# Two chunks' shift and exponential in one operation each, in the second attention layer of a fused kernel

## The chip, the cores and the metric

The kernel runs on one core of one Trainium2 chip. The metric is the time on the device in microseconds, as the median of several runs. One profiled execution per kernel stands beside it; its span runs from the first to the last instruction. In views of the profile, PE is the matrix engine (TensorE), PEld its loading of weights, DVE is VectorE, ACT is ScalarE, POOL is GpSimd and SP is the engine whose queue issues most DMAs. L944 is line 944 of the kernel before.

## The reference

The input x has two images of 256 channels and 64 x 64 places, in fp32. Two attention layers follow each other. The change lies in the second one ("layer 1"), which takes the first one's output:

```python
def _L1_conv_ref(x, w_qkv, b_qkv, w_out, b_out):
    import jax
    import jax.numpy as jnp
    HEADS = 4
    b, c, h, w = x.shape
    head_dim = c // HEADS
    qkv = jnp.einsum('oc,bchw->bohw', w_qkv, x) + b_qkv[None, :, None, None]
    qkv = qkv.reshape(b, HEADS, 3 * head_dim, h * w)
    q, k, v = jnp.split(qkv, 3, axis=2)
    scale = 1.0 / jnp.sqrt(jnp.asarray(head_dim, x.dtype))
    attn = jax.nn.softmax(jnp.einsum('bhdn,bhdm->bhnm', q, k) * scale, axis=-1)
    out = jnp.einsum('bhnm,bhdm->bhnd', attn, v).reshape(b, c, h, w)
    return jnp.einsum('oc,bchw->bohw', w_out, out) + b_out[None, :, None, None] + x
```

There are 4 heads of 64 channels and 4,096 places, so each head of each image has a 4,096 x 4,096 matrix of scores, which goes through a softmax along the keys. Layer 0 is an attention of the same kind with 4 heads of 16 channels, a normalisation ahead of it and a gate behind it.

## The kernel before

**Tiling.** Layer 1 works in 32 units: two images, two pairs of heads, and eight blocks of 512 queries. A unit runs over 32 chunks of 128 keys. For each chunk, keys lie along the partitions, and a tile of 128 x (2 heads x 512 queries) holds the scores. A step handles two chunks, so a unit has 16 steps and the layer 512. A unit is cut into two halves of 16 chunks (8 steps): each half has its own maximum per query, its own values' sums and its own sum of weights, and the two are joined at the end.

**The path of one chunk.** PE multiplies keys by queries into a pair of PSUM banks (`score`, L861). There are two such pairs, so the scores of a step's first chunk and of its second chunk each reuse the pair of the same chunk of the step before. VectorE takes the running maximum with the pair (`keep`, L878), and ScalarE copies the pair into an SBUF tile of 128 x 1024 fp32, called `raw` (L879). When a half is done, its maximum is turned across the partitions by PE (`turn_max`, L886), reduced by VectorE (`fold`, L898), split by GpSimd into three bf16 numbers (`split`, L909 to L916), turned back (`turn`, L925) and spread over all partitions in one pair of PSUM banks (`spread_shift`, L939). From then on, each chunk of the half gets this negative maximum added by VectorE in place (`shift`, L944), goes through the exponential on ScalarE in place (in `weigh`, L956), is added into the sum of weights by GpSimd (also in `weigh`, L966 for the first addition of a half and L968 for the others), and is multiplied by the values on PE (`gather`, L978). The last ten odd chunks (and two even ones) get their sums of weights on PE instead (L988).

**The delay.** `LAG` is 10 steps: a chunk's shift comes 10 steps after its scores. The even chunk is shifted and weighed in the same step; the odd chunk is shifted at that step's end and weighed at the next one's beginning. Both are gathered 11 steps after their scores. The `raw` tiles live in a ring of 24 (2 x LAG + 4).

**The order.** All of it is written out by hand: `seq` keeps instructions in program order, so each engine's queue is the order in which the loop at L1219 to L1247 issues. A step first issues the scores of both chunks, then the weights of the old odd chunk, then the first chunk's maximum and copy, the even chunk's shift and weights, then the second chunk's maximum and copy, then the values' sums of two chunks, and last the odd chunk's shift. Other work hangs at named places of a step ("start", "early", "early end", "late", "late end") through `at` (L1109 to L1156): the projections of the next queries and of the next keys and values (the latter for 24 of the 32 units, kept in DRAM in between), the turning of maxima at steps 0 and 8 of a unit, the sums of weights, factors and rows of the unit before at steps 12 to 14, and the output projection of the first image. After the last scores, `fetch_last`, `last_output` and `project_half` bring x and the attention rows in and form the second image's output.

The core of a step, with the middle left out:

```python
            if 0 <= t - LAG - 1 < END:
                weigh(pair[1] - 2 * LAG - 2)
...
            if inside:
                keep(pair[0], scores[0])
            if behind:
                shift(pair[0] - 2 * LAG)
                weigh(pair[0] - 2 * LAG)
...
            if inside:
                keep(pair[1], scores[1])
```

Of the kernel before, what the change touches and what calls it, by code (L numbers as in the profile page):

```python
# [27 lines left out]
def conv_attention_kernel(  # L28
# [216 lines left out]
    with own0:  # L245
# [155 lines left out]
        def maxima(x, g):  # L401

            u = b, j = units0[x // NM]
            m, i = divmod(x % NM, PB)
            if u not in mxs:
                mxs[u] = small.tile([P, PB * H, NJ], F32, tag="mx0", name=f"mx0_{b}_{j}")
            for h in (2 * g, 2 * g + 1):
                r = slice(32 * h, 32 * h + 32)
                ps = bank(f"a0_{b}_{j}_{x % NM}_{h}")
                seq(nc.tensor.matmul(  # L410
                    ps, qs0[u][r, bass.ts(i, P)], kTs[b][r, bass.ts(m, NB)],
                    start=True, stop=True,
                ))
                seq(nc.vector.tensor_reduce(mxs[u][:, i * H + h, m : m + 1], ps, AX.X, ALU.max))  # L414
# [363 lines left out]
    with (  # L778
# [4 lines left out]
        tc.tile_pool(name="psm", bufs=1, space=PSUM) as psm,  # L783
    ):
        own_ring = ExitStack()
        ring = own_ring.enter_context(tc.tile_pool(name="ring", bufs=2 * LAG + 4))
        small_bank[0] = lambda name: psm.tile([P, NB], F32, tag="misc", name=name)
        rmax, negs, mrows, shifts, raws, accs = {}, {}, {}, {}, {}, {}
        avs1, srows, losts, joined, halves = {}, {}, {}, {}, {}
        rts = [None, None]  # L790
        outs = {}
        halves_of = {}
        kd, vd = (
# [73 lines left out]
        def keep(t, ps):  # L867

            u = b, g, j = units[t // NM]
            m = t % NM  # L870
            raw = ring.tile([P, 2, NB], F32, tag="raw", name=f"raw_{b}_{g}_{j}_{m}")
            raws[t] = raw
            n = m // GS
            if m > 0:
                before = raws[t - 1] if m == 1 else rmax[u, (m - 1) // GS]
                if (u, n) not in rmax:
                    rmax[u, n] = l1.tile([P, 2, NB], F32, tag="rmax", name=f"rmax_{b}_{g}_{j}_{n}")
                seq(nc.vector.tensor_tensor(rmax[u, n], ps, before, ALU.max))  # L878
            seq(nc.scalar.copy(raw, ps))  # L879
# [61 lines left out]

        def shift(t):
            u = units[t // NM]
            seq(nc.vector.tensor_tensor(  # L944
                raws[t], raws[t], shifts[u, t % NM // GS], ALU.add
            ))

        def on_tensor(t):
            return t >= LATE and (t % 2 == 1 or t < LATE + 4)
# [1 line left out]
        def weigh(t):  # L951
            u = b, g, j = units[t // NM]
            m = t % NM
            n = m // GS
            p = raws[t]
            seq(nc.scalar.activation(p, p, AF.Exp, scale=D1**-0.5))  # L956

            if on_tensor(t):
                return
            if (u, n) not in first:  # L960
                first[u, n] = p
            elif (u, n) not in accs:
                accs[u, n] = l1.tile(
                    [P, 2, NB], F32, tag="acc", bufs=3, name=f"acc_{b}_{g}_{j}_{n}"
                )
                seq(nc.gpsimd.tensor_tensor(accs[u, n], first[u, n], p, ALU.add))  # L966
            else:
                seq(nc.gpsimd.tensor_tensor(accs[u, n], accs[u, n], p, ALU.add))  # L968
# [43 lines left out]

        def keep_total(u):
            b, g, j = u
            row = l1.tile([P, NB], F32, tag="srow", bufs=1, name=f"srow_{b}_{g}_{j}")
            seq(nc.scalar.copy(row, srows[u]))
            srows[u] = row
            seq(nc.scalar.activation(losts[u], losts[u], AF.Exp, scale=D1**-0.5))
# [78 lines left out]
                )  # L1097

        def fetch_output(b, j):
            fetch(("xo", b, j), x1[b][j], "xo", 2, l1)  # L1100
            fetch(("ao", b, j), att[b][:, bass.ts(j, NB)], "ao", 1, l1)


# [5 lines left out]
        for n, u in enumerate(units):  # L1109
            b, g, j = u  # L1110
            t0 = n * US
            if n > 0:
                at(t0 - 5, "start", lambda u=u, b=b, j=j: fetch(("q", u), x1[b][j]))
                at(t0 - 2, "late", lambda u=u: next_queries(u, 0))
                at(t0 - 1, "early", lambda u=u: next_queries(u, 1))
                at(t0 - 1, "early end", lambda u=u: keep_queries(u))
            if n < len(units) - NJ:
                to = (*units[n + NJ][:2], j)
                at(t0 + 1, "start", lambda to=to: fetch(("kv", *to), x1[to[0]][to[2]]))
                for c in range(CC):  # L1120
                    at(t0 + 4 + c, "early", lambda to=to, c=c: next_keys(*to, c))
                at(t0 + 5, "early end", lambda to=to: store_keys(*to))
                at(t0 + 6, "early", lambda to=to: next_values(*to, 0))
                at(t0 + 7, "early", lambda to=to: next_values(*to, 2))
                at(t0 + 7, "early end", lambda to=to: store_values(*to))

                t1 = (n // NJ * NJ + NJ - 1) * US
                at(t1 + 2 * j + 2, "start", lambda to=to: load_keys(*to))
                at(t1 + 2 * j + 3 + LAG, "start", lambda to=to: load_values(*to))
            for k in range(NG):  # L1130
                t1 = t0 + (k + 1) * GS // 2
                at(t1, "early", lambda u=u, k=k: turn_max(u, k, 0))
                at(t1, "early end", lambda u=u, k=k: fold(u, k, 0))
                at(t1, "late", lambda u=u, k=k: turn_max(u, k, 1))
                at(t1, "late end", lambda u=u, k=k: (fold(u, k, 1), split(u, k)))
                at(t1 + 1, "late", lambda u=u, k=k: turn(u, k))
                at(t1 + 2, "early", lambda u=u, k=k: spread_shift(u, k))
            t1 = t0 + US + GS // 2
            at(t1 + 4, "early", lambda u=u: total(u))
            at(t1 + 4, "early end", lambda u=u: keep_total(u))  # L1140
            at(t1 + 5, "early", lambda u=u: turn_total(u))
            at(t1 + 5, "early end", lambda u=u: factors(u))
            at(t1 + 5, "late", lambda u=u: turn_sums(u, 1))
            at(t1 + 5, "late end", lambda u=u: rows(u, 1))
            at(t1 + 6, "early", lambda u=u: turn_sums(u, 0))
            at(t1 + 6, "early end", lambda u=u: rows(u, 0))
            if b < B - 1 and (g, j) == (PR - 1, NJ - 1):
                for i in range(NJ):
                    t1 = t0 + US + (i + 4) * GS // 2
                    at(t1, "start", lambda b=b, i=i: fetch_output(b, i))  # L1150
                    for o in range(CC):
                        at(
                            t1 + 3 + 4 * o, ("early", "late")[o],
                            lambda b=b, i=i, o=o: project_out(b, i, o, misc(f"o1_{b}_{i}_{o}")),
                        )
                        at(t1 + 3 + 4 * o, "late end", lambda b=b, i=i, o=o: output(b, i, o))  # L1156
# [5 lines left out]
        def fetch_last(i):  # L1162

            b = B - 1
            tag, bufs, pool = (("xb", 3, l1x), ("xo", 2, l1), ("ao", 1, l1))[(i >= 3) + (i >= 5)]
            t = pool.tile([P, CC, NB], F32, tag=tag, bufs=bufs, name=f"x_last_{i}")
            nc.sync.dma_start(out=t, in_=x1[b][i].rearrange("(c p) n -> p c n", p=P))
            last_x.append(t)
# [7 lines left out]
        def last_output():  # L1176
# [7 lines left out]
                r, n = k * D1, D1 - NB // D1  # L1184
                nc.sync.dma_start(out=a[r : r + n, :], in_=att[b][P + r : P + r + n, :])
            last_att.append(a)
            for i in range(NJ - 2, NJ):
                t = tail.tile([P, CC, NB], F32, tag=f"xo{i}", name=f"x_last_{i}")
                nc.sync.dma_start(out=t, in_=x1[b][i].rearrange("(c p) n -> p c n", p=P))
                last_x.append(t)  # L1190
# [14 lines left out]
                    seq(nc.vector.tensor_tensor(x, ps[:, o, :], x, ALU.add))  # L1205

        own_tail = ExitStack()
        for i in range(NJ - 2):
            at(END - 12 + 2 * i, "start", lambda i=i: fetch_last(i))
        at(END, "start", lambda: fetch_first_half())  # L1210
        at(END + LAG, "late end", lambda: last_output())


        FILL = {
# [4 lines left out]
        for t in range(max(t for t, _ in extras) + 1):  # L1219
            inside, behind = 0 <= t < END, 0 <= t - LAG < END  # L1220
            pair = (2 * t, 2 * t + 1)
            scores = [score(c) for c in pair] if inside else []
            if 0 <= t - LAG - 1 < END:
                weigh(pair[1] - 2 * LAG - 2)
            hung(t, "start")
            hung(t, "early")
            for j in FILL.get((t, "early"), ()):
# [2 lines left out]
                keep(pair[0], scores[0])  # L1230
            if behind:
                shift(pair[0] - 2 * LAG)
                weigh(pair[0] - 2 * LAG)
            hung(t, "early end")
            for j in FILL.get((t, "early end"), ()):
                project_half(j, 0, first_half[j])
            if inside:
                keep(pair[1], scores[1])
            if 0 <= t - LAG - 1 < END:
                for c in pair:  # L1240
                    gather(c - 2 * LAG - 2)
            hung(t, "late")
            hung(t, "late end")
            for j in FILL.get((t, "late end"), ()):
                project_half(j, 0, first_half[j])
            if behind:
                shift(pair[1] - 2 * LAG)  # L1247
        assert not extras
        for j in range(NJ):
            project_half(j, 1, last_att[0][:, bass.ts(j, NB)])  # L1250
# [54 lines left out]
```

## Time and profile before

| | |
|---|---|
| median of 3 runs | 4,742.67 us (4,740.17 to 4,742.81) |
| the profiled execution | 4,741.58 us, span 4,739.8 us |
| busy over the span | PE 96%, DVE 83%, ACT 72%, POOL 54% |
| 2,900 to 3,100 us, of 200 us | PE 188.5, DVE 187.9, ACT 169.1, POOL 185.0 |
| layer 1's shifts, L944 | 1,024 of 1,213 ns |
| layer 1's exponentials, L956 | 1,024 of 1,062 ns |
| layer 1's sums of weights, L968 | 884 of 2,373 ns |

A line of a group has the program's line, the engine and the operation, the output and the inputs by name, their shapes (partitions x elements) and how many there are; then the busy time in us and the mean of one in ns; then how long the engine stood idle just before them, and which engine and line ended most of that. A line of a timeline has the start in us from the span's start, the duration, and the idle time just before it with what ended it. Consecutive instructions on VectorE overlap a little in these records (a start every 1.13 us at 1.22 us of duration), so distances between starts are safer than sums of durations. A PE row of "x4" or "x8" is a run of that many instructions.

### The profile page before, as it was taken

Reading aid. Unit: us, or ns where it says so; the run is one execution under the profiler, and the core shown is the slowest. Engines: PE = TensorE matmul, PEld = TensorE weight load, DVE = VectorE, ACT = ScalarE, POOL = GpSimd, SP = SyncE. Lnnn points to the kernel's source line nnn. Section 1 sums busy time; section 2 is a strip of 40 time slices with the busy share of each in tenths; the row PEclk is TensorE's granted clock in tenths of the full one; section 3 lists DMA queues with packets and bytes.
Section 4 is the critical chain, followed back from the end, with each engine's and each line's share of the span. In section 5 each row is a group of like instructions: output and inputs, shape, how many; then the busy total and the mean of one; then the engine's idle time right before and its main releaser. Section 6 shows DMA issues by size and latency. Waiting matters only on the chain.

```text
span 4739.8 us, 70643 instructions
## 1 busy us (share of the span) xinstructions
PE 4526.9 (96%) x27506; PEld 1496.2 (32%) x27506; DVE 3917.0 (83%) x4584; ACT 3394.1 (72%) x4508; POOL 2540.6 (54%) x1491
## 2 busy tenths in 40 slices
PE   8999999999999999989999999999999999999998
PEld 3433333333333333333232232323233332222222
DVE  6777777777777777359999999999999899999996
ACT  3366666666666666668888888888887778888884
POOL 6300000000000000039999999999998889999994
PEclk9999999999999999999999999999999999999999
DMA  3100000000000000110000100001111111000002
GB/s 103 34 4 19 19 21 15 15 15 15 15 15 15 15 13 13 57 63 25 23 25 17 54 30 23 25 23 36 52 36 45 63 52 47 18 14 7 14 16 74
DMA packets 113381, 140.10 MB, mean 30 GB/s; under 512 B 51864, under 2 KB 52696, under 8 KB 112932
## 3 DMA queue, kind: packets, MB, share of 16 engines
q1 hardware_dynamic: 111260, 135.11, 9.2%
q8 instruction: 216, 3.54, 0.3%
q14 instruction: 121, 0.99, 0.1%
q10 hardware_dynamic: 1784, 0.46, 0.0%
HBM read 93.58 MB, written 41.70 MB: 29 GB/s over the span
## 4 chain that ended last, share of the span: by engine, by line
PE 58%; DVE 15%; POOL 15%; issue 6%; ACT 5%; DMA 1%; SPq 0%; ACTq 0%; DVEq 0%; POOLq 0%
PE s L448 24%; POOL acc L968 13%; PE av L463 12%; DVE rmax L878 10%; PE s L861 6%; PE av L978 5%; DVE raw L944 4%; ACT raw L879 4%; PE a L410 2%; PE p L270 1%; PE k1p L672 1%; POOL acc L966 1%; PE rt L886 1%; PE q1p L672 1%; PE o L549 1%
## 5 line engine op out<-in xcount | busy, mean ns | idle before, releaser
L968 POOL TENSOR_TENSOR acc<-acc,raw 128x1024 f32<-128x1024 f32 x884 | 2098.1, 2373 | 89.4 <-ACT raw L956 30.2
L414 DVE TENSOR_REDUCE mx<-a 128x1 f32<-128x512 f32 x2048 | 1315.3, 686 | 450.5 <-PE a L410 449.4
L451 ACT ACTIVATE p<-s 128x512 f32<-128x512 f32 x2048 | 1109.8, 597 | 701.3 <-PE a L410 367.3
L944 DVE TENSOR_TENSOR raw<-raw,shift 128x1024 f32<-128x1024 f32 x1024 | 1238.0, 1213 | 19.2 <-PE shift L939 12.7
L861 PE MATMUL s<-q,k 64*128 64x512 f32 x4096 | 1117.2, 636 | 142.9 <-ACT raw L879 134.6
L878 DVE TENSOR_TENSOR rmax<-s,rmax 128x1024 f32<-128x1024 f32 x960 | 1170.1, 1219 | 72.7 <-PE s L861 70.8
L879 ACT COPY raw<-s 128x1024 f32<-128x1024 f32 x1024 | 1037.7, 1013 | 259.4 <-DVE rmax L878 173.5
L448 PE MATMUL s<-q,kT 32*128 32x512 f32 x4096 | 1219.1, 640 | 0.0
L956 ACT ACTIVATE raw<-raw 128x1024 f32<-128x1024 f32 x1024 | 1086.9, 1062 | 178.4 <-DVE raw L944 147.3
L410 PE MATMUL a<-kT,q 32*128 32x512 f32 x4096 | 1129.7, 643 | 1.2 <-DVE mx L414 1.0
L978 PE MATMUL av<-raw,v 128*64 128x512 f32 x4096 | 999.3, 606 | 2.0
L463 PE MATMUL av<-p,v 128*32 128x256 f32 (+1 forms) x7904 | 650.2, 399 | 0.6 <-ACT avs L477 0.6
L861 PEld LDWEIGHTS s<-q,k 64*128 64x128 f32 x4096 | 317.1, 185 | 827.9 <-ACT raw L879 628.0
L513 POOL TENSOR_TENSOR f<-f,dyn 128x16 f32<-128x16 f32 x15 | 3.3, 223 | 1028.2 <-DVE f L512 1028.2
L448 PEld LDWEIGHTS s<-q,kT 32*128 32x128 f32 x4096 | 397.9, 183 | 426.3 <-issue 392.1
L978 PEld LDWEIGHTS av<-raw,v 128*64 128x64 f32 x4096 | 243.3, 136 | 587.6 <-issue 428.8
L463 PEld LDWEIGHTS av<-p,v 128*32 128x32 f32 x7904 | 157.6, 108 | 751.5 <-issue 737.3
L564 POOL TENSOR_SCALAR res<-res 128x1024 f32<-128x1024 f32 x16 | 16.8, 1049 | 660.5 <-ACT res L563 660.5
L410 PEld LDWEIGHTS a<-kT,q 32*128 32x128 f32 x4096 | 305.0, 184 | 31.4 <-DVE mx L414 18.2
L966 POOL TENSOR_TENSOR acc<-raw,raw 128x1024 f32<-128x1024 f32 x64 | 152.4, 2381 | 112.7 <-ACT raw L956 103.8
L898 DVE TENSOR_REDUCE negs<-rt 128x4 f32<-128x512 f32 x128 | 88.3, 690 | 50.1 <-PE rt L886 47.6
L318 DVE RECIPROCAL std<-std 128x128 f32<-128x128 f32 x64 | 56.1, 920 | 37.7 <-ACT std L313 37.7
(332 smaller groups left out, 1840.4 us busy)
## 6 DMA issues: line engine op xcount, KB each, us to landing
x<-in_x_dram SPq DMA_DIRECT2D x16, 512.0 KB
res<-in_x_dram SPq DMA_DIRECT2D x16, 512.0 KB
x<-res SPq DMA_DIRECT2D x16, 512.0 KB
att<-rows SPq DMA_DIRECT2D x62, 128.0 KB
kd<-k1s SPq DMA_DIRECT2D x24, 256.0 KB
vd<-v1s SPq DMA_DIRECT2D x24, 256.0 KB
k<-kd SPq DMA_DIRECT2D x24, 256.0 KB
v<-vd SPq DMA_DIRECT2D x24, 256.0 KB
```

The costliest lines, as they stand in the source:

```text
L410: seq(nc.tensor.matmul(ps, qs0[u][r, bass.ts(i, P)], kTs[b][r, bass.ts(m, NB)], start=True, stop=True,))
L414: seq(nc.vector.tensor_reduce(mxs[u][:, i * H + h, m : m + 1], ps, AX.X, ALU.max))
L448: seq(nc.tensor.matmul(ps, kTs[b][r, bass.ts(m, P)], qs0[u][r, :], start=True, stop=True))
L451: seq(nc.scalar.activation(pt[:, k, :], ps, AF.Exp, scale=D0**-0.5))
L463: seq(nc.tensor.matmul(avs[u][32 * h : 32 * h + 32, cols], vs0[b][:, m, 32 * h : 32 * h + 32], pts[t, h // 2][:, h % 2, cols], start=(m == ...
L861: seq(nc.tensor.matmul(ps[:, k, :], ks[b, g, m // PB][r, bass.ts(m % PB, P)], qs1[u][r, :], start=True, stop=True,))
L878: seq(nc.vector.tensor_tensor(rmax[u, n], ps, before, ALU.max))
L879: seq(nc.scalar.copy(raw, ps))
L944: seq(nc.vector.tensor_tensor(raws[t], raws[t], shifts[u, t % NM // GS], ALU.add))
L956: seq(nc.scalar.activation(p, p, AF.Exp, scale=D1**-0.5))
L968: seq(nc.gpsimd.tensor_tensor(accs[u, n], accs[u, n], p, ALU.add))
L978: seq(nc.tensor.matmul(avs1[u, n][k * D1 : (k + 1) * D1, :], v[:, m % PB, k, :], raws[t][:, k, :], start=(m % GS == 0), stop=(m % GS == GS ...
```

## The change

Two neighbouring `raw` tiles become one tile of 128 x 2 x 1024, of which `keep` fills one half for each chunk. The ring holds 13 such pairs (LAG + 3). `shift` adds the negative maximum to both chunks in one VectorE operation, with the PSUM operand repeated by a stride of zero; a new function `exponentials` takes the exponential of both in one ScalarE operation. The shift of the pair stands where the even chunk's stood; behind it, the exponential and the two additions of weights belong to the pair that was shifted one step earlier. The values' sums come one step later, 12 steps behind the scores. Values are loaded, and the last output begins, one step later for that.

Room for the ring comes from other buffers: layer 0's maxima move to a pool that closes with layer 0 (two buffers, as before), the row of sums shares the keys' and values' two buffers, and the x block of the output has one buffer instead of two. So the last x blocks that are fetched early are five instead of six, and three instead of two are fetched in the tail.

```diff
-                mxs[u] = small.tile([P, PB * H, NJ], F32, tag="mx0", name=f"mx0_{b}_{j}")
+                mxs[u] = l0w.tile([P, PB * H, NJ], F32, tag="mx0", name=f"mx0_{b}_{j}")
...
-        ring = own_ring.enter_context(tc.tile_pool(name="ring", bufs=2 * LAG + 4))
+        ring = own_ring.enter_context(tc.tile_pool(name="ring", bufs=LAG + 3))
...
-            raw = ring.tile([P, 2, NB], F32, tag="raw", name=f"raw_{b}_{g}_{j}_{m}")
-            raws[t] = raw
+            if t % 2 == 0:
+                both = ring.tile([P, 2, 2, NB], F32, tag="raw", name=f"raw_{b}_{g}_{j}_{m}")
+                raw_pairs[t] = both
+                raws[t], raws[t + 1] = both[:, 0], both[:, 1]
+            raw = raws[t]
...
-            seq(nc.vector.tensor_tensor(
-                raws[t], raws[t], shifts[u, t % NM // GS], ALU.add
-            ))
+            both = raw_pairs[t]
+            by = shifts[u, t % NM // GS].unsqueeze(1).to_broadcast([P, 2, 2, NB])
+            seq(nc.vector.tensor_tensor(both, both, by, ALU.add))
+
+        def exponentials(t):
+            both = raw_pairs.pop(t)
+            seq(nc.scalar.activation(both, both, AF.Exp, scale=D1**-0.5))
...
-            seq(nc.scalar.activation(p, p, AF.Exp, scale=D1**-0.5))
...
-            row = l1.tile([P, NB], F32, tag="srow", bufs=1, name=f"srow_{b}_{g}_{j}")
+            row = l1.tile([P, NB], F32, tag="kv", name=f"srow_{b}_{g}_{j}")
...
-            fetch(("xo", b, j), x1[b][j], "xo", 2, l1)
+            fetch(("xo", b, j), x1[b][j], "xo", 1, l1)
...
-                at(t1 + 2 * j + 3 + LAG, "start", lambda to=to: load_values(*to))
+                at(t1 + 2 * j + 4 + LAG, "start", lambda to=to: load_values(*to))
...
-            for i in range(NJ - 2, NJ):
+            for i in range(NJ - 3, NJ):
...
-        at(END + LAG, "late end", lambda: last_output())
+        at(END + LAG + 1, "late end", lambda: last_output())
...
-            if 0 <= t - LAG - 1 < END:
-                weigh(pair[1] - 2 * LAG - 2)
+            old = pair[0] - 2 * LAG - 2 if 0 <= t - LAG - 1 < END else None
...
                 shift(pair[0] - 2 * LAG)
-                weigh(pair[0] - 2 * LAG)
+            if old is not None:
+                exponentials(old)
+                weigh(old)
+                weigh(old + 1)
...
-            if 0 <= t - LAG - 1 < END:
-                for c in pair:
-                    gather(c - 2 * LAG - 2)
+            if 0 <= t - LAG - 2 < END:
+                gather(pair[0] - 2 * LAG - 4)
+                gather(pair[1] - 2 * LAG - 4)
...
-            if behind:
-                shift(pair[1] - 2 * LAG)
```

More of the change, by code (lines that the diff above doesn't have):

```diff
@@ L790, in conv_attention_kernel @@
         rts = [None, None]
+        raw_pairs = {}
         outs = {}
@@ L1164, in fetch_last @@
             b = B - 1
-            tag, bufs, pool = (("xb", 3, l1x), ("xo", 2, l1), ("ao", 1, l1))[(i >= 3) + (i >= 5)]
+            tag, bufs, pool = (("xb", 3, l1x), ("xo", 1, l1), ("ao", 1, l1))[(i >= 3) + (i >= 4)]
             t = pool.tile([P, CC, NB], F32, tag=tag, bufs=bufs, name=f"x_last_{i}")
@@ L1207, in conv_attention_kernel @@
         own_tail = ExitStack()
-        for i in range(NJ - 2):
+        for i in range(NJ - 3):
             at(END - 12 + 2 * i, "start", lambda i=i: fetch_last(i))
         at(END, "start", lambda: fetch_first_half())
-        at(END + LAG, "late end", lambda: last_output())
+        at(END + LAG + 1, "late end", lambda: last_output())
         FILL = {
```

## The prediction

> **What bounds the kernel now.** The change touches layer 1, from about 2,100 us to the end. I read its costliest groups on the page first (busy us, mean ns of one, then idle time just before them and its main releaser):
>
> ```profile
> L968 POOL TENSOR_TENSOR acc<-acc,raw 128x1024 f32<-128x1024 f32 x884 | 2098.1, 2373 | 89.4 <-ACT raw L956 30.2
> L944 DVE TENSOR_TENSOR raw<-raw,shift 128x1024 f32<-128x1024 f32 x1024 | 1238.0, 1213 | 19.2 <-PE shift L939 12.7
> L861 PE MATMUL s<-q,k 64*128 64x512 f32 x4096 | 1117.2, 636 | 142.9 <-ACT raw L879 134.6
> L878 DVE TENSOR_TENSOR rmax<-s,rmax 128x1024 f32<-128x1024 f32 x960 | 1170.1, 1219 | 72.7 <-PE s L861 70.8
> L879 ACT COPY raw<-s 128x1024 f32<-128x1024 f32 x1024 | 1037.7, 1013 | 259.4 <-DVE rmax L878 173.5
> L956 ACT ACTIVATE raw<-raw 128x1024 f32<-128x1024 f32 x1024 | 1086.9, 1062 | 178.4 <-DVE raw L944 147.3
> ```
>
> Three of them wait in a ring: scores for the copy that empties their PSUM pair, the copy for the maximum of the same pair, the maximum for scores. Second, busy time by stretch (length, then PE, PEld, DVE, ACT, POOL):
>
> ```profile
> 2700.00:2900.00 200.00, 188.79 (x808) 60.75 (x810) 187.82 (x176) 169.11 (x180) 186.49 (x101) 1.00 0.10 31
> 4300.00:4500.00 200.00, 184.44 (x786) 55.26 (x784) 191.21 (x184) 170.97 (x181) 190.88 (x107) 1.00 0.05 12
> ```
>
> PE, VectorE and GpSimd are all at 92 to 96%: no engine stands alone, so the order in which they hand work to each other counts as much as the work. Third, therefore, the timeline of one engine at a time, over two steps (start us, duration us, idle before):
>
> ```profile
> 2628.66 1.13 PE L861 MATMUL s<-q,k 64*128 64x512 f32 x4
> 2630.24 1.13 PE L861 MATMUL s<-q,k 64*128 64x512 f32 x4 [0.45 <-ACT raw L879]
> 2631.29 1.13 PE L672 MATMUL k1p<-xb_('kv', 0, 1, 7)_22535,w 128*128 128x512 f32 x2
> 2632.35 1.94 PE L978 MATMUL av<-raw,v 128*64 128x512 f32 x8
> 2634.22 1.99 PE L861 MATMUL s<-q,k 64*128 64x512 f32 x8
> ```
>
> ```profile
> 2627.86 1.22 DVE L878 TENSOR_TENSOR rmax<-s,rmax 128x1024 f32<-128x1024 f32 x1
> 2628.99 1.21 DVE L944 TENSOR_TENSOR raw<-raw,shift 128x1024 f32<-128x1024 f32 x1
> 2630.12 1.22 DVE L878 TENSOR_TENSOR rmax<-s,rmax 128x1024 f32<-128x1024 f32 x1
> ...
> 2635.39 1.22 DVE L878 TENSOR_TENSOR rmax<-s,rmax 128x1024 f32<-128x1024 f32 x1 [0.66 <-PE s L861]
> 2636.53 1.21 DVE L944 TENSOR_TENSOR raw<-raw,shift 128x1024 f32<-128x1024 f32 x1
> 2637.66 1.22 DVE L878 TENSOR_TENSOR rmax<-s,rmax 128x1024 f32<-128x1024 f32 x1
> ```
>
> ```profile
> 2629.17 1.01 ACT L879 COPY raw<-s 128x1024 f32<-128x1024 f32 x1
> ```
>
> The reader is to see one **loop of two steps** in these rows. Second maximum of a step (2627.86), its copy (2629.17), the second scores of the next step, which reuse that pair (2630.24), the keys' projection, the values' sums (2632.35), the first scores of the step after (2634.22), their maximum (2635.39), a shift (2636.53), the second maximum (2637.66): 9.80 us, or 8.74 without the projection's 1.06. VectorE alone needs four starts of 1.13 us in a step, 9.04 in two. In a plain step VectorE wins (4.52 a step); where PE has a side job the loop wins, and the 0.66 us of idle VectorE is that.
>
> **What the Trainium skill says.** "VectorE: DVE Perf Modes", section on the TRN2 errata, gives an fp32 tensor_tensor (N+151)/0.96 ns: 1,224 for N = 1024, where this trace has 1,213 and 1,219; and 2,291 for N = 2048, of which the trace has none. "PSUM — Partial Sum Buffer", section on bank collisions, says that two engines may not read one bank and quadrant together and that accesses are ordered across engines for it: here every such copy starts 1.31 us or more after its maximum does, as if one needed the other's result. "Perfetto Trace Analysis", section on optimizing Scalar/DVE operations, holds both sides: larger operations help a saturated engine, and breaking instructions up helps where an engine causes bubbles on others. The trace shows VectorE in both roles.
>
> **The change part by part.**
>
> *Shift of a pair in one operation.* Two starts of 1.13 us become one of 1.13 + 1024/0.96 GHz = 2.20. At most 2.26 (nothing saved), at least 2.13 (all start cost gone). It saves VectorE 0.06 a step, 502 steps with a shift (10 to 511): 30 us, if VectorE were the bound.
>
> *Its place.* Before, the even chunk's shift stands between the two maxima and the odd one behind both. Now the whole pair stands between them. The loop passes from first to second maximum, so it gets 2.20 − 1.13 = **1.07 longer: 8.74 + 1.07 = 9.81 for two steps, 4.91 a step**, above VectorE's own 1.13 + 2.20 + 1.13 = 4.46. The second shift stood off the loop, and is now on it.
>
> *Exponentials, one step later.* A pair takes 1.06 + 1024 at 1.2 GHz = 1.92, at most 2.12. They no longer wait for a shift (147 us of waits go), but stand between the two copies: first copy at 1.31 behind the first maximum, exponential 0.97 later, done at 1.31 + 0.97 + 1.9 = 4.2 behind it; the second copy is due at 1.13 + 2.20 + 1.31 = 4.64. So 0.45 us of cover; ScalarE's side copies (0.5 to 0.7 us: k, v, q, sums) behind the exponential overrun it by about 0.1 to 0.2. The saved waits are hidden anyway.
>
> *Values' sums one step later.* Free: PE no longer waits for a fresh exponential; its order and length stay.
>
> *Ring of 13 pairs.* A first copy reuses the pair of 13 steps before, whose exponential ended about 6.9 us before that copy (two steps of 4.91 and 1.31 + 1.17, less 1.17 + 4.2). GpSimd's two sums take 2 x 2.44; about 2 us of slack are left. I take 0; if the rows' extra 2.6 us on GpSimd eat it, up to 2 us a unit.
>
> *Moved buffers.* Same counts for the layer 0 maxima: 0. The row of sums in the keys' buffers: its predecessors are five steps old, 0. One output buffer in place of two: on SP's queue the next fetch waits for a write, 1 to 4 us, three steps (15 us) before use, and nothing behind it on that queue is due sooner: 0. Keys' and values' loads a step later: as their readers, 0.
>
> *The sum, per unit (16 steps).* Units now: the sums' first small operation starts at 2596.59 and 2677.89, so 81.3 us with projections of the next keys; without, five units from 4219.94 to 4616.09 take 79.2. After: eight loops of 9.81 are 78.5. PE's side work in a unit (transposes and spreading 5.4, k 2.1, v 2.2, q 2.1, totals 1.0) is 12.8; a loop meets PE in every other step, so half, 6.4. VectorE's side work ahead of a second maximum (two reductions of 0.6, factors 0.5, rows 0.6) is 2.3: half, 1.15. A unit's first chunk has no maximum: −0.57. That is 85.5. Then places where the loop changes parity or waits for a third engine: the transposition of the maxima waits for GpSimd's split behind two sums (now up to 1.10 in the trace, twice a unit: 2.0), new queries behind the longer exponential (0.65), bank hand-over at the rows (0.3): 3.0. Walking one unit step by step with the same distances gave starts of 0, 5, 11, 15, 21, 27, 32, 38, 43, 49, 55, 59, 65, 70, 76, 82 and 88.4. **88.4 − 81.3 = 7.1 us a unit**; without projections both lose about 2.1, so it stays. 502/16 = 31.4 units: 223 us.
>
> *The end.* After the last scores PE works off the pairs left; one more is 1.87 + 0.98 = 2.9. A third x block is fetched only then, and VectorE waits for it ahead of the last rows: the first block lands 12 us after issue now; I take 4, between 0 and 6. Together 7.
>
> The profiled execution took 4,741.58 us (span 4,739.8, 1.8 around it), 1.1 below the median. 4,741.6 + 223 + 7 = 4,971.6, so **4,971**.
>
> **The rivals.**
> *A, the loop as above:* 4,971; own range 4,920 to 5,020 (5.5 to 8.6 us a unit). Chance 0.70. For it: its distances are all in one excerpt, and the loop already shows there.
> *B, side work falls into slack.* PE now idles about 0.9 us in a plain step, and if most of the side jobs hide there, a unit is 78.5 + 6 to 7, some 3.5 longer: 110 + 7, 4,859. Against: scores wait in PE's order, so a job ahead of them moves them. 0.10.
> *C, GpSimd's bursts hold the ring,* 2 us a unit more: 63, so 5,034. GpSimd is 95% busy now, but a longer step gives it rest. 0.08.
> *D, faster:* VectorE stays the bound. Then the fewer starts give 30 us less, 7 back at the end: 4,719. It decides as soon as the loop is under VectorE's 4.46 a step, that is if second scores need not wait for the second copy, by 0.45 us. For it: VectorE's 95%. Against: 0.45 us of that very wait stand in the plain step above. 0.09. That the longer operations merely trade places, near 4,742: 0.03.
>
> **How the numbers follow.** B to C leave out D and the even case, 0.12, and halves of B and C: 4,860 to 5,030. About 0.2%, 9.5 us, is what a measurement here can tell from no change: faster 0.09, same 0.03, slower 0.88.
>
> **What would show it.** Right: L944 and L956 512 times at 2.29 and 1.9 us; plain steps 4.9 apart in place of 4.52; maxima waiting for scores rising from 71 us to several hundred; VectorE's and GpSimd's shares falling to some 85%; copies waiting for maxima, not for GpSimd. Wrong: VectorE still back to back (D); plain steps of 4.9 with side jobs that add nothing (B); first copies released by GpSimd (C); a pair's shift well off 2.2.

## The result, and the profile after

The changed kernel takes **4,964.97 us** (median of 4 runs, 4,963.61 to 4,971.23) against 4,741.93 us of the kernel before on the same chip: a ratio of 1.0474, 95% interval 1.046 to 1.0488. It is slower by 223 us; the prediction said 4,971.

The same groups on the page of the changed kernel. Lines have moved: L862 is the scores, L882 the maximum, L883 the copy, L950 the shift, L954 the exponential, L975 the sums of weights.

```profile
L975 POOL TENSOR_TENSOR acc<-acc,raw 128x1024 f32<-128x1024 f32 x884 | 2093.2, 2368 | 403.0 <-ACT raw L954 359.5
L883 ACT COPY raw<-s 128x1024 f32<-128x1024 f32 x1024 | 1036.7, 1012 | 749.8 <-DVE rmax L882 711.2
L882 DVE TENSOR_TENSOR rmax<-s,rmax 128x1024 f32<-128x1024 f32 x960 | 1171.0, 1220 | 312.3 <-PE s L862 300.1
L862 PE MATMUL s<-q,k 64*128 64x512 f32 x4096 | 1135.3, 641 | 271.3 <-ACT raw L883 243.3
L950 DVE TENSOR_TENSOR raw<-raw,shift 128x2048 f32<-128x2048 f32 x512 | 1166.1, 2279 | 8.9 <-PE shift L943 7.8
L954 ACT ACTIVATE raw<-raw 128x2048 f32<-128x2048 f32 x512 | 979.2, 1914 | 1.0 <-DVE raw L950 1.0
```

Each wide operation does what was asked of it: 512 shifts cost VectorE 1,166 us in place of 1,238, 512 exponentials cost ScalarE 979 in place of 1,087, and the exponentials' waits for shifts (147 us) are gone. The time is lost in the three rows that wait in a ring: copies for maxima 711 us (174 before), maxima for scores 300 (71), scores for copies 243 (135). GpSimd now waits more as well (the additions of L975 360 us for exponentials; the same group had 30 before, and a half's first additions, L966, another 104). So every engine's share falls in the table by stretches (the same two as before):

```profile
2700.00:2900.00 200.00, 174.84 (x750) 54.73 (x750) 174.19 (x128) 149.22 (x131) 170.11 (x97) 1.00 0.12 35
4300.00:4500.00 200.00, 169.17 (x710) 50.71 (x704) 175.65 (x130) 147.85 (x127) 174.52 (x98) 0.98 0.03 8
```

And VectorE's timeline over two plain steps, with no side work on VectorE or PE (ScalarE has one small copy of 0.59 us in it):

```profile
4547.86 1.22 DVE L882 TENSOR_TENSOR rmax<-s,rmax 128x1024 f32<-128x1024 f32 x1 [0.60 <-PE s L862]
4549.01 2.28 DVE L950 TENSOR_TENSOR raw<-raw,shift 128x2048 f32<-128x2048 f32 x1
4551.20 1.22 DVE L882 TENSOR_TENSOR rmax<-s,rmax 128x1024 f32<-128x1024 f32 x1
4552.87 1.22 DVE L882 TENSOR_TENSOR rmax<-s,rmax 128x1024 f32<-128x1024 f32 x1 [0.46 <-PE s L862]
4554.02 2.28 DVE L950 TENSOR_TENSOR raw<-raw,shift 128x2048 f32<-128x2048 f32 x1
4556.21 1.22 DVE L882 TENSOR_TENSOR rmax<-s,rmax 128x1024 f32<-128x1024 f32 x1
4557.62 1.22 DVE L882 TENSOR_TENSOR rmax<-s,rmax 128x1024 f32<-128x1024 f32 x1 [0.19 <-PE s L862]
```

The shift takes 2.19 us from its start to the second maximum's, and VectorE idles for scores ahead of every first maximum. Two steps take 4557.62 − 4547.86 = 9.76 us, where the loop had been summed to 9.81, and the old kernel had 9.04. The rest of the loop, on ScalarE and PE in the same stretch:

```profile
4552.45 1.01 ACT L883 COPY raw<-s 128x1024 f32<-128x1024 f32 x1 [0.43 <-DVE rmax L882]
4553.52 1.13 PE L862 MATMUL s<-q,k 64*128 64x512 f32 x4 [1.10 <-ACT raw L883]
4554.58 1.94 PE L985 MATMUL av<-raw,v 128*64 128x512 f32 x8
4556.44 1.13 PE L862 MATMUL s<-q,k 64*128 64x512 f32 x4
```

From the second maximum (4551.20) to its copy it is 1.25 us, then 1.07 to the second scores of the next step, 1.06 to the values' sums, 1.86 to the first scores of the step after, 1.18 to their maximum (4557.62); 1.15 to the shift and 2.19 to the second maximum close the loop: 9.76. GpSimd's two additions happen to take as long as half of it (4.88 us, from starts 2.44 apart), but they don't set the pace here: GpSimd idled 2.86 and 0.17 us for exponentials ahead of the two pairs that it adds in this stretch.

### The profile page after: what moved, and what is told of

Read it like the earlier page. It is cut to its first block, busy times and chain, and to the rows that moved or that the text cites. A ratio compares the mean times of both kernels' runs of the same rounds, so it can differ in the third digit from the quotient of the medians.

```text
span 4961.8 us, 68957 instructions
## 1 busy us (share of the span) xinstructions
PE 4553.6 (92%) x27506; PEld 1502.1 (30%) x27506; DVE 3909.8 (79%) x4072; ACT 3281.9 (66%) x3996; POOL 2533.3 (51%) x1491
## 4 chain that ended last, share of the span: by engine, by line
PE 61%; DVE 12%; POOL 10%; ACT 9%; issue 5%; DMA 1%; SPq 0%; ACTq 0%; DVEq 0%; POOLq 0%
PE s L448 23%; PE av L463 12%; PE s L862 10%; POOL acc L975 9%; DVE rmax L882 8%; PE av L985 6%; ACT raw L883 4%; ACT raw L954 4%; DVE raw L950 3%; PE a L410 2%; PE p L270 1%; PE v1p L705 1%; PE k1p L672 1%; PE q1p L672 1%; PE o L549 1%
## 5 line engine op out<-in xcount | busy, mean ns | idle before, releaser
L975 POOL TENSOR_TENSOR acc<-acc,raw 128x1024 f32<-128x1024 f32 x884 | 2093.2, 2368 | 403.0 <-ACT raw L954 359.5
L883 ACT COPY raw<-s 128x1024 f32<-128x1024 f32 x1024 | 1036.7, 1012 | 749.8 <-DVE rmax L882 711.2
L882 DVE TENSOR_TENSOR rmax<-s,rmax 128x1024 f32<-128x1024 f32 x960 | 1171.0, 1220 | 312.3 <-PE s L862 300.1
L862 PE MATMUL s<-q,k 64*128 64x512 f32 x4096 | 1135.3, 641 | 271.3 <-ACT raw L883 243.3
L950 DVE TENSOR_TENSOR raw<-raw,shift 128x2048 f32<-128x2048 f32 x512 | 1166.1, 2279 | 8.9 <-PE shift L943 7.8
L954 ACT ACTIVATE raw<-raw 128x2048 f32<-128x2048 f32 x512 | 979.2, 1914 | 1.0 <-DVE raw L950 1.0
L862 PEld LDWEIGHTS s<-q,k 64*128 64x128 f32 x4096 | 315.5, 186 | 972.9 <-ACT raw L883 689.5
L410 PEld LDWEIGHTS a<-kT,q 32*128 32x128 f32 x4096 | 304.9, 183 | 31.5 <-DVE mx L414 18.2
L973 POOL TENSOR_TENSOR acc<-raw 128x1024 f32<-128x1024 f32 x63 | 148.5, 2357 | 13.8 <-ACT raw L954 12.7
L929 PE MATMUL nm1p<-ident,negmax 128*128 128x128 bf16 x256 | 25.4, 222 | 74.6 <-POOL negmax L916 74.6
```

The costliest lines, as they stand in the source:

```text
L410: seq(nc.tensor.matmul(ps, qs0[u][r, bass.ts(i, P)], kTs[b][r, bass.ts(m, NB)], start=True, stop=True,))
L862: seq(nc.tensor.matmul(ps[:, k, :], ks[b, g, m // PB][r, bass.ts(m % PB, P)], qs1[u][r, :], start=True, stop=True,))
L950: seq(nc.vector.tensor_tensor(both, both, by, ALU.add))
L954: seq(nc.scalar.activation(both, both, AF.Exp, scale=D1**-0.5))
```

## The experiments

All but the last change the order or the width of operations alone; the last changes what the maximum reads. All compute everything. Each was timed beside the kernel before, which stayed at 4,741.7 to 4,742.4 us. The distance between the first scores of one step and the next, averaged over units, is used below as "the step"; "the last units" are the 26th to the 31st, which have no projections of keys and values.

**Both shifts between the maxima, in the kernel before.** The place alone:

```diff
             if behind:
                 shift(pair[0] - 2 * LAG)
+                shift(pair[1] - 2 * LAG)
                 weigh(pair[0] - 2 * LAG)
...
-            if behind:
-                shift(pair[1] - 2 * LAG)
```

> The kernel before with one edit: the odd chunk's shift moves from the end of the step to right behind the even one's, between the two maxima; both stay single operations, exponentials, values' sums and ring as before. Loop theory (the second shift between the maxima lengthens the two-step loop through PE, VectorE and ScalarE): loop 8.74 + 1.13 = 9.87 us for two steps, 4.93 a step in place of 4.52, so about 4,975 us (4,940 to 5,010). Rival (the loss comes from the wide operations, the later exponentials and values' sums or the ring): nothing of that is in here, so 4,740 to 4,780.

Measured: 4,978.94 us, ratio 1.05 (1.0482 to 1.0517). This one moved line costs 237 us, and nothing else of the change is in this kernel. VectorE's timeline:

```profile
4304.91 1.23 DVE L878 TENSOR_TENSOR rmax<-s,rmax 128x1024 f32<-128x1024 f32 x1 [0.56 <-PE s L861]
4306.05 2.34 DVE L944 TENSOR_TENSOR raw<-raw,shift 128x1024 f32<-128x1024 f32 x2
4308.31 2.55 DVE L878 TENSOR_TENSOR rmax<-s,rmax 128x1024 f32<-128x1024 f32 x2
4310.77 2.34 DVE L944 TENSOR_TENSOR raw<-raw,shift 128x1024 f32<-128x1024 f32 x2
4313.03 1.22 DVE L878 TENSOR_TENSOR rmax<-s,rmax 128x1024 f32<-128x1024 f32 x1
4314.78 1.23 DVE L878 TENSOR_TENSOR rmax<-s,rmax 128x1024 f32<-128x1024 f32 x1 [0.53 <-PE s L861]
```

Two steps are 9.87 us, the sum that was expected. ("x2" is two instructions back to back.) The place alone makes a loss of the size that the whole change has. Whether the width, the lateness or the ring add to it is left to the runs below.

**Two single shifts in the wide one's place, in the changed kernel.** The width alone:

```diff
-            both = raw_pairs[t]
-            by = shifts[u, t % NM // GS].unsqueeze(1).to_broadcast([P, 2, 2, NB])
-            seq(nc.vector.tensor_tensor(both, both, by, ALU.add))
+            for c in (t, t + 1):
+                seq(nc.vector.tensor_tensor(
+                    raws[c], raws[c], shifts[u, t % NM // GS], ALU.add
+                ))
```

> The changed kernel with two single shifts, one behind the other, in the place of the wide one; all else as changed. Loop theory: place counts, not width: the loop is 2 x 1.13 - 2.20 = 0.06 us longer for two steps, so 4,965 to 4,995 us. Rival W (the width of the shift is the cost): a good part of the loss goes, 4,750 to 4,900.

Measured: 4,983.17 us, 18 above the changed kernel (its two runs lie 10 us apart). So the width of the shift isn't the cost; it saves a little.

**Two single exponentials in the wide one's place.** The loop in `exponentials` runs over both chunks.

> The changed kernel with two single exponentials, one behind the other, in the place of the wide one. Loop theory: 0.45 us of cover stand behind the exponential, two single ones take about 0.1 more: no change, 4,960 to 4,975 us. Rival (a pair's exponential holds GpSimd's additions back, since both chunks come at once): single ones let the first addition start 0.9 us sooner, and 20 to 60 us come back, 4,905 to 4,945.

Measured: 4,958.68 us, ratio 1.0462 (1.0444 to 1.0479), an interval that overlaps that of the changed kernel; the median is 1 us below the range expected. The width of the exponential is not the cost either, and the burst of two additions holds back next to nothing.

**The exponential ahead of the first copy, shift between the maxima.**

```diff
             scores = [score(c) for c in pair] if inside else []
...
+            if old is not None:
+                exponentials(old)
+                weigh(old)
+                weigh(old + 1)
             hung(t, "start")
...
-            if old is not None:
-                exponentials(old)
-                weigh(old)
-                weigh(old + 1)
```

> The changed kernel with the wide exponential and the additions behind it moved to the start of the step, ahead of the first copy; the wide shift stays between the maxima. Loop theory: from first maximum to second copy the shift's path is 1.13 + 2.20 + 1.31 = 4.64 us, the exponential no longer stands in it, so the loop stays 9.81 for two steps; only its side work (ScalarE's small copies behind the exponential, GpSimd's split, which waits for sums that now start sooner) gets less: 4,900 to 4,965. Rival E (after the run with the shift last, 5,047, and the one with the exponential first, 4,784: the exponential's place between the copies is the cost, and the shift's place is little): 4,760 to 4,830.

Measured: 4,958.9 us, ratio 1.0459 (1.0441 to 1.0476). While the wide shift stands between the maxima, it covers the exponential; moving that away gives at most a few us. Rival E is out for the changed kernel.

**The wide shift last.** The same kernel with the shift moved behind the second maximum, once with the exponential left between the copies, once with it first, once behind the second copy:

```diff
-            if behind:
-                shift(pair[0] - 2 * LAG)
...
             for j in FILL.get((t, "late end"), ()):
                 project_half(j, 0, first_half[j])
+            if behind:
+                shift(pair[0] - 2 * LAG)
```

> The changed kernel with the wide shift moved to the end of the step, behind the second maximum; the wide exponential stays between the two copies. Loop theory: the shift leaves the loop, and what stands next in it is the wide exponential ahead of the second copy: 1.31 + 0.97 + 1.9 us from first maximum to second copy, then 1.07 + 1.06 + 1.87 + 1.17 back to a first maximum, 9.3 for two steps, 4.65 a step in place of 4.91: about 4,840 us (4,800 to 4,880). Rival W (a wide operation costs by its width, wherever it stands): 4,950 or more. Rival O (only VectorE's order counts): 4,690 to 4,740.

> As the run with the shift last, and the wide exponential, with the additions of weights behind it, moves from between the copies to the start of the step, ahead of the first copy. Loop theory: from first maximum to second copy now 0.1 + 1.9 + 0.97, loop 8.1 for two steps, 4.07 a step, below VectorE's 4.46 and GpSimd's 4.88; GpSimd's 78.3 us a unit are the bound, with some waits 79 to 80: about 4,700 us (4,670 to 4,740), faster than before. Rival W (wide operations cost by their width): slower than before, 4,760 or more.

> The kernel with the wide shift last, and the wide exponential behind the second copy, so out of the loop but later. Loop theory: VectorE's 1.33 + 1.13 + 2.20 = 4.66 bound a plain step as with the exponential first, but a pair reaches GpSimd some 3.5 us later and its two additions (4.9) end just when the ring needs the pair: first copies waiting for GpSimd appear, 4,790 to 4,900. Rival E' (any place but the first is as bad as between the copies): 5,000 or more.

| shift | exponential | us | ratio (95%) |
|---|---|---|---|
| between the maxima (as changed) | between the copies | 4,964.97 | 1.0474 (1.046 to 1.0488) |
| between the maxima | first | 4,958.9 | 1.0459 (1.0441 to 1.0476) |
| last | between the copies | 5,046.88 | 1.0643 (1.0622 to 1.0664) |
| last | first | 4,783.75 | 1.0088 (1.0073 to 1.0103) |
| last | behind the second | 5,045.16 | 1.0641 (1.062 to 1.0662) |

All three expectations missed, all too low, and each time the measured value lies where the rival had put it (4,950 or more, 4,760 or more, 5,000 or more). These three times alone would speak for the rivals. That the width isn't the cost is decided by the two single shifts in the place between the maxima (above) and in the last place (below): both are slower than the wide one. What held: taken out of both chains (shift last, exponential first) the wide pair loses 42 us to the kernel before, not 223. What did not: I had VectorE at 4.46 us a step. Its timeline with the shift last and the exponential first says 4.66:

```profile
4303.58 2.55 DVE L882 TENSOR_TENSOR rmax<-s,rmax 128x1024 f32<-128x1024 f32 x2
4306.04 2.28 DVE L950 TENSOR_TENSOR raw<-raw,shift 128x2048 f32<-128x2048 f32 x1
4308.24 1.22 DVE L882 TENSOR_TENSOR rmax<-s,rmax 128x1024 f32<-128x1024 f32 x1
```

Two maxima in a row take 2.55 us at 1.22 each, so the second starts 1.33 after the first, where a maximum and a shift of the same size side by side start 1.13 apart (the prediction's excerpt), and two shifts as well (2.34 for two in the timeline of the first experiment). The second reads the running maximum that the first wrote. One wide shift a step leaves two maxima side by side somewhere, and the 0.2 us eat the 0.06 that the width saves three times over.

The two runs with the exponential later show a second thing. With it behind the second copy, steps without side work take what was summed: 4.66 us at steps 6 and 7 of the last units. With it between the copies they do so only in part: 4.66 and 4.68 at steps 5 and 7, but 5.27 and 4.94 at steps 4 and 6, so 9.8 us for two steps on average where 9.3 were summed. And where GpSimd's split of the maxima is due, the kernel with the exponential behind the second copy takes 10.3 us at step 1 of a unit and 9.7 at step 9 (5.0 and 5.6 in the kernel before). The waits of the two kernels between 2,150 and 4,650 us (total, times, longest), first with the exponential behind the second copy:

```profile
PE nm1p L929 <- POOL negmax L916: 225.9, 55, 4.6
ACT raw L883 <- POOL acc L975: 61.6, 75, 1.2
```

and with it between the copies:

```profile
ACT raw L883 <- POOL acc L975: 98.7, 33, 3.7
PE nm1p L929 <- POOL negmax L916: 91.3, 55, 2.2
```

The changed kernel has 65.9 and 8.7 us there. PE stands in its queue for a split that GpSimd reaches only behind two additions of 2.4 us each; and copies find the ring full. With the exponential behind the second copy, a plain step of 4.66 us is shorter than GpSimd's two additions, 4.88, so GpSimd falls behind in plain steps; that the pair's later arrival leaves less of the ring to absorb this is argued, not shown. For that kernel the split accounts for most of the loss: steps 1 and 9 alone are 9.5 us a unit above the kernel before, of 11.4 in the last units. So the rival's number came true, but not in the plain steps. For the kernel with the exponential between the copies the split does not account for it: its steps 12 to 15 take 25.3 us in the last units against 21.9 with the exponential first, and no run took those apart.

**Single shifts in their old places, with the pair's wide exponential.** Even chunk between the maxima, odd chunk at the step's end, all the rest as changed; once with the exponential between the copies, once first. A last run on top of the second puts the second of a pair's additions at the end of the step, behind the split:

```diff
-            both = raw_pairs[t]
-            by = shifts[u, t % NM // GS].unsqueeze(1).to_broadcast([P, 2, 2, NB])
-            seq(nc.vector.tensor_tensor(both, both, by, ALU.add))
+            seq(nc.vector.tensor_tensor(
+                raws[t], raws[t], shifts[u, t % NM // GS], ALU.add
+            ))
...
+            if behind:
+                shift(pair[1] - 2 * LAG)
```

> The changed kernel with single shifts in the places of the kernel before (even chunk between the maxima, odd chunk at the end of the step); the wide exponential of the pair stays between the copies, a step later. Loop theory: from first maximum to second copy it is 1.13 + 1.13 + 1.31 = 3.57 us over VectorE but 1.31 + 0.97 + 1.9 = 4.18 over the exponential, so the exponential sets the loop: 9.3 for two steps, about 4,845 us (4,800 to 4,890). Rival (the exponential's place is free, as my prediction had it while the wide shift covered it): 4,740 to 4,765.

Measured: 4,936.6 us, ratio 1.041 (1.039 to 1.0431), 92 above the middle of the expectation: the exponential between the copies is anything but free once no wide shift covers it (the next run, which moves it alone, is 203 us faster). As above, the direction was right and the size too small.

> The run with single shifts in the places of the kernel before (odd one at the end of the step), with the wide exponential at the start of the step; values' sums a step later and the ring of pairs as changed. Loop theory: loop 8.74 again, VectorE's four starts of 1.13 bound a plain step at 4.53; if two maxima in a row, each needing the other's result, start 1.33 apart (as the runs with the shift last show, 4.66 and 4.72 a step), a shift between them saves 0.2 us a step against two single shifts last: about 4,808 - 502 x 0.19 = 4,715, with the waits at the unit's side work 4,715 to 4,765. Rival (later exponentials, later values' sums or the ring cost by themselves): 4,790 or more.

Measured: 4,733.2 us, ratio 0.9983 (0.9976 to 0.999). Against the run with the exponential first and the wide shift between the maxima (4,958.9 us), only the shifts differ, and 226 us go: this is the place of the pair's second shift again, now in the changed kernel. Against the two single shifts last (next run) only the even chunk's shift stands elsewhere, between the two maxima, and 75 us come back of the 95 that 502 steps of 0.19 would give: the side-by-side maxima cost most of what their distance says. Later values' sums, a wide exponential a step late and the ring of 13 pairs together cost nothing on balance, so they are out as the cause of the loss.

> The kernel with the shift last and the exponential first, but with two single shifts in the place of the wide one. What the width alone is worth when VectorE is close to the bound: 0.06 us a step, 502 steps, at most 30 us; with GpSimd as the bound 0 to 15. Loop theory: 0 to 30 us above the same kernel with the wide shift, and still below the kernel before. Rival W (width costs): faster than the wide one.

Measured: 4,808.03 us, ratio 1.0139 (1.0124 to 1.0154), 24 above the wide shift in the same place, as expected. But neither of the two is below the kernel before, as the expectation had it: this one is 66 us above. Here, with the shift off the chain, the width is worth 0.05 us a step, close to the 0.06 of the sum.

> The kernel with single shifts in their old places and the wide exponential first, with one more edit: of a pair's two additions of weights, the second goes to the end of the step on GpSimd's queue, so that at steps 0 and 8 of a unit the split of the maxima stands between the two and not behind both. Loop theory with GpSimd near its bound: PE's waits for the split in that kernel (48 us on matmuls, up to 1.7 us at a time) shrink, since the split comes up to 2.4 us sooner; but GpSimd has only some 1.2 us a unit left to its 78.3, so at most about 35 us come: 4,695 to 4,733, a little below. Rival (the split's waits cost nothing, GpSimd or VectorE's own work sets the unit): 4,725 to 4,742, no change.

```diff
                 exponentials(old)
                 weigh(old)
-                weigh(old + 1)
...
+            if old is not None:
+                weigh(old + 1)
             if behind:
                 shift(pair[1] - 2 * LAG)
```

Measured: **4,722.52 us, ratio 0.9959 (0.9945 to 0.9972): faster than both kernels**, by 0.4% against the kernel before. The expectation held, but 11 us came of the 35 that it allowed, and its rival began only 2.5 us higher. The weights' load for the transposition waited 102.1 us for the split without this edit,

```profile
PEld L929 <- POOL negmax L916: 102.1, 58, 2.5
```

and with it

```profile
PEld L929 <- POOL negmax L916: 6.5, 8, 0.8
```

The matmuls' own waits for it, 48.0 us without the edit, are gone. A unit without projections takes 78.7 us (79.5 without the edit, 79.2 in the kernel before), and GpSimd stands idle for only 1.2 of them (0.60 and 0.57 in the unit from 4,560 us on).

**The maximum from the copy.** In the changed kernel, the copy goes ahead of the maximum, which then reads SBUF only:

```diff
-                seq(nc.vector.tensor_tensor(rmax[u, n], ps, before, ALU.max))
-            seq(nc.scalar.copy(raw, ps))
+                seq(nc.scalar.copy(raw, ps))
+                seq(nc.vector.tensor_tensor(rmax[u, n], raw, before, ALU.max))
+            else:
+                seq(nc.scalar.copy(raw, ps))
```

> The changed kernel with the copy ahead of the maximum, and the maximum taken from the copy in SBUF instead of from the PSUM pair; so VectorE no longer stands between scores and the release of their pair. Loop theory: the loop is left with ScalarE (1.17 + 0.97 + 1.9) and PE (1.07 + 1.06 + 1.87), 8.05 for two steps, so the shift's place between the maxima costs nothing: about 4,700 us if a maximum of two SBUF operands takes what it took and GpSimd is not slowed. If GpSimd and such a maximum hinder each other at SBUF, GpSimd's additions (2.37 us) show it, and the time can be anywhere up to 5,600. Rival (the wide shift itself is the cost): 4,950 or more with GpSimd's additions unchanged.

Measured: 5,599.3 us, in a single run. The lines of its page (L977 is the sum of weights, L883 the maximum):

```profile
L977 POOL TENSOR_TENSOR acc<-acc,raw 128x1024 f32<-128x1024 f32 x884 | 2600.5, 2942 | 276.7 <-ACT raw L956 222.7
L883 DVE TENSOR_TENSOR rmax<-raw,rmax 128x1024 f32<-128x1024 f32 x960 | 2034.4, 2119 | 111.2 <-ACT raw L882 74.7
```

The maximum takes 2.12 us in place of 1.22, and GpSimd's addition 2.94 in place of 2.37. Each slows the other: the 34 maxima of this trace that ran while GpSimd stood idle took 1.22 us each, and the 490 that ran beside it almost throughout 2.90 on average; the 27 additions beside which no such maximum ran took 2.36. So VectorE can't be taken out of the loop this way, and the run says nothing for or against the loop.

## Why the prediction was right, point by point

**The place of the shift.** The step that carried the forecast, 1.07 us more in a loop of two steps, is shown: by the plain steps after (9.76 us for two, summed 9.81), by the one moved line in the kernel before (9.87 summed and measured, 4,978.94 us), and by the width, which changes 18 us in that place and not more. With single shifts in their old places and the exponential first, all the rest of the change loses nothing (4,733.2 us).

**Unit and layer.** From the first step with a shift (10) to the last step's scores, the kernel before took 2,556.6 us and the changed one 2,771.8: 215 more, 6.9 a unit, where the sum had 223 and 7.1. The walk through a unit holds step by step: in the units with projections that the trace repeats (the 3rd to the 18th), steps start at 0, 5.0, 10.7, 15.0, 20.7, 26.4, 31.5, 37.2, 42.4, 48.2, 54.1, 58.2, 64.3, 69.8, 75.5, 82.1 and 88.1, at most 0.9 us off. That half of PE's side work enters is shown: steps 4 to 7 take 21.7 us with the projections of keys and values and 19.5 without, 2.1 us for 4.3 us of matmuls. So rival B, side work that falls into slack, is out.

**Third engines.** The split holds PE 73 us on 62 occasions (22 on 34 before): 1.2 us each, 2.4 a unit, where I had 2.0. New queries hold PE's scores 20 us on 27 occasions: 0.74 each, where I had 0.65. Copies wait 8.7 us for GpSimd in all, so rival C, the ring, is out for this kernel; it showed only where the step got shorter.

**The end.** From the last step's first score to the end of the span it is 98.9 us, 90.9 before: 8.0, where I had 7. VectorE waits 6.6 us for the third x block ahead of the last rows (3.5 for an x block in the kernel before, so 3.1 of it are new, where I took 4):

```profile
4926.35 1.41 DVE L1208 SCALAR_TENSOR_TENSOR x_last<-o,bo,x_last 128x512 f32<-128x512 f32 x2 [6.62 <-DMA x_last<-x]
```

**Luck.** That the total came within 6 us is better than its parts: 215 us for 223 in the units and 8.0 for 7 at the end, against an own range of 50 us either way.

**Wrong in it.** VectorE's own work in a step was put at 1.13 + 2.20 + 1.13 = 4.46 us; with two maxima side by side it is 4.66. In the changed kernel the loop is longer than either, so it did no harm to the forecast. But rival D was worth less than I said: with VectorE as the bound a plain step is 4.66 us, above the old 4.52, and not 30 us below. The same term stood in the later expectation of 4,700 us, which came out at 4,784; it wasn't the only error there, since that expectation named GpSimd as the bound. Two readings of the kernel before were off as well. Copies start 1.25 us or more after their maximum and not 1.31: 51 of 992 come sooner than 1.305. And the 0.9 us of idle PE in a plain step, under rival B, are those of the kernel to come (0.96 at steps 5 to 7 of the last units); the kernel before has 0.45 there.

**A duration and an advice.** The duration of a 2,048-element shift, 2,291 ns by "VectorE: DVE Perf Modes", section on the TRN2 errata, is 2,279 in the trace. ScalarE's second 1,024 elements took 1,914 − 1,062 = 852 ns, as the prediction's 1.2 GHz has it. The advice in "Perfetto Trace Analysis", section on optimizing Scalar/DVE operations, to break up instructions where an engine that isn't saturated causes bubbles on others, fits this case only in part: the wide shift broken up in its place made the kernel 18 us slower. What helped is that two single shifts can stand in different places: with the exponential first in both, VectorE idles 243 us for scores with the wide shift between the maxima and 75 with single shifts in their old places, and PE's scores wait 326 and 121 us for copies.

**Open.** Why the kernel with the shift last and the exponential between the copies is as slow as 5,047 us is explained only in part. That the 1.33 us between neighbouring maxima come from the one needing the other's result is argued from the program and the distances; no run changed that dependence alone. The traces speak for it: two shifts side by side, which also read PSUM, start 1.13 us apart, and in the kernel before the small sums (L1036 and L1038), each of which reads what the line before it wrote, start 0.03 us after its end, where neighbours with no shared result overlap by 0.08.

## What to carry to other kernels

Before two operations are joined, write down the loop that passes a buffer from engine to engine, and ask which of the two stood on it: the joined one stands there whole. The start cost that it saves (here 0.06 us on VectorE, 0.2 on ScalarE) is worth something only on an engine that sets the pace, and the longer operation may also have been what kept two dependent operations apart. A wide operation belongs where nothing waits behind it: here the pair's exponential at the start of the step, with the shifts left single, ran level with the kernel before (0.2% faster), and with one addition moved 0.4% faster. That the exponential's width, and not only its place, is part of that gain was not tried.

## What the runs showed of the hardware that I had not expected

Two VectorE maxima of 128 x 1,024 in a row on the same running maximum start 1.33 us apart, independent neighbours of the same size 1.13.

A maximum with both operands in SBUF takes 2.12 us while GpSimd adds (1.22 with one operand in PSUM), and GpSimd's addition then takes 2.94 us (2.37). "GPSIMD Engine Reference", section on specifications, says that GpSimd shares its SBUF interfaces with VectorE and contends with VectorE operations that have two SBUF inputs; the run agrees and gives the size, as the maxima beside an idle GpSimd show.

The two kernels with the longest repeated waits of PE in layer 1 (4.6 us at a time for the split, and 6.1 for a maximum) were granted the lowest mean clocks, 0.963 (5,045 us) and 0.935 (5,599); the kernel before had 0.996, the changed one 0.992. A score matmul takes 674 and 694 ns on average there, 636 and 641 here. It is a tendency and no more: the kernel at 5,047 us waited up to 2.4 us and had 0.980, the one at 4,937 up to 2.9 and had 0.989, and which of waits and clock brings about the other was not tested.
